# LayerNorm's statistics move from VectorE to TensorE and ScalarE, with a new order of work, in a two-layer image kernel

## The chip, the cores and the metric

The kernel runs on one core of a Trainium2 chip. The time is device microseconds of one execution, median of three runs. The engines are named as in the profile: PE (TensorE matmul), PEld (its weight load), DVE (VectorE), ACT (ScalarE), POOL (GpSimd) and SP (SyncE, which here only issues DMAs).

## The reference

Input x is four images of 192 channels x 128 x 128, float32. Two layers, each `x = x + f(groupnorm(x))`, with 32 groups of 6 channels. (The code calls them `layer0` and `layer1`; the text says layer 1 and layer 2.)

Layer 1: a 1x1 convolution to 48 channels; 16 of them go through a fractional Fourier transform, 16 through a real FFT, both with small convolutions on magnitude and phase; then a 1x1 convolution back to 192. Layer 2 is a state-space layer over the 16384 pixels of an image as a sequence:

```python
seq = (seq - mu) * rsqrt(var + 1e-5) * ln_g + ln_b        # over 192 channels
xs, z = split(seq @ in_proj_w.T, 2)                       # 384 and 384
u  = silu(causal_conv4(xs) + conv_b)
dt, Bm, Cm = split(u @ x_proj_w.T, [12, 28])              # 12, 16, 16
dt = softplus(dt @ dt_proj_w.T + dt_proj_b)
h[t] = h[t-1] * exp(dt[t] * A) + (dt[t] * u[t]) * Bm[t]   # 384 x 16 states
y = sum_s(h * Cm) + u * Dp
out = (y * silu(z)) @ out_proj_w.T
```

## The kernel before

**Layer 1.** `analysis(b)` loads an image in 16 pieces of 768 KB (`load`, L199), takes group statistics with `bn_stats` (L205), keeps the last 4 pieces, loads the other 12 again, multiplies by the scaled 1x1 weights (L301), evacuates (L305) and writes the result to DRAM (L311). `forward` reads it back with one DMA (L317) and transforms, `backward` transforms back, `synthesis` projects to 192 channels, adds x and writes `xmid` (L506, L510, L514). `weave` interleaves the four for different images. Image 0's analysis runs alone first. The last image's synthesis is interleaved with layer 2's prelude, two of its positions for one piece.

**Layer 2.** 128 chunks of 512 tokens (32 an image). A chunk has 24 positions: three tiles j of 128 channels times eight groups of two states. In each position `scans` (L977 on) runs two scans on DVE (L989), h = da*h + db. Then POOL multiplies both states of h by c (L1002, tile hc), and PE adds them up over the states while transposing (L1015, `sums`, three positions later). A DMA saves the last column of h (carry, L1000). The decay da = exp(dt*A) is ACT's (L911), made AHEAD states in advance. The input db = dt*u*B is made in one of three ways, set in KINDS for each position: V, a DVE product from PSUM (L932); O, a POOL product (L943), for which the decay goes to PSUM; P, ACT scales a transposed tile (L960, `scale`) and PE transposes it back (L975).

The rest of a chunk's work (normalization, convolution, projections, loads, gate, output) is put at fixed places by PLAN: an entry (-31, "A", "moments", 0) is done 31 positions before its chunk's first scan, in phase A of that position. A position's phases are S, A, M, L; the two scans begin after A, M lies between them, L after the carry. All queues work in order, so PLAN is the order written out by hand. SP's queue holds in this order the loads `load_b` and `load_c` (rows of B and C broadcast to 128 partitions, one buffer for each group), `load_x`, `load_xr`, the carries and the output. PSUM banks are handed out first in, first out (`psum`, `done`).

Normalization: `to_tokens` (L717) turns 512 tokens x 192 channels by a matmul with a diagonal matrix gd that holds the group norm's scale, and its shift in a 97th row that meets a row of ones in xm. `moments` (L732, L734) takes mean and variance on DVE from PSUM, `rstd` (L741 to L744) is Ln and two Exp on ACT (the second into PSUM for DVE), `shift` (L749) is DVE's -mean*rstd, and `normed` (L758) applies both on ACT. `group_norm` (L641 to L652) makes gd per image; the shift's row goes out to a DRAM tile and comes back as a row. `to_channels` and `channels` (L768, L784) turn back, and a DMA (L790) puts channels 128 to 191, moved by one token, into partitions 64 to 127 for the convolution (`conv`, L799). `proj_z` (L805, L806) computes z with two matmuls for each j; the second has 64 rows of weights and 64 of zeros.

## Time and profile before

| | us |
|---|---|
| median of 3 runs (10828.12 to 10840.17) | 10829.38 |
| profiled execution | 10830.13 |
| its span | 10828.4 |
| busy: PE, DVE, ACT, POOL | 9879.0, 10219.2, 9404.2, 9214.5 |
| first scan starts, last scan ends | 1395.10, 10811.20 |
| three costliest groups: POOL L1002, DVE L989 (first form), ACT L911 (first form) | 7202.9, 5821.6, 3423.7 |

The page gives busy time as a union: instructions that overlap by their pipelines count once. Start-to-start distances in a timeline are what an instruction really takes of a full engine. A line of waits is: engine and what waited, what released it, us in total, times, longest. A line of groups is: line, engine, operation, tiles, shape, count, busy us, mean ns. A timeline line is: start us, duration us, engine, line, operation, tiles and shape, count, and in brackets the idle time before it with what ended it. SPq and ACTq are queue issues.

### The profile page before, as it was taken

Reading aid. Unit: us, or ns where it says so; the run is one execution under the profiler, and the core shown is the slowest. Engines: PE = TensorE matmul, PEld = TensorE weight load, DVE = VectorE, ACT = ScalarE, POOL = GpSimd, SP = SyncE. Lnnn points to the kernel's source line nnn. Section 1 sums busy time; section 2 is a strip of 40 time slices with the busy share of each in tenths; the row PEclk is TensorE's granted clock in tenths of the full one; section 3 lists DMA queues with packets and bytes.
Section 4 is the critical chain, followed back from the end, with each engine's and each line's share of the span. In section 5 each row is a group of like instructions: output and inputs, shape, how many; then the busy total and the mean of one; then the engine's idle time right before and its main releaser. Section 6 shows DMA issues by size and latency. Waiting matters only on the chain.

```text
span 10828.4 us, 170277 instructions
## 1 busy us (share of the span) xinstructions
PE 9879.0 (91%) x55538; PEld 6942.9 (64%) x55538; DVE 10219.2 (94%) x11587; ACT 9404.2 (87%) x19559; POOL 9214.5 (85%) x4214
## 2 busy tenths in 40 slices
PE   4776789999999999999999999999999999999998
PEld 2444366666666666666666666666666666666666
DVE  4666699999999999999999999999999999999999
ACT  1332189999999999999999999999999999999998
POOL 0000089999999999999999999999999999999999
PEclk8888799999999999999999999999999999999999
DMA  8786743443443443443444444444444344344343
GB/s 229 189 227 179 222 137 108 126 127 108 127 124 111 124 125 112 122 126 112 120 127 113 118 127 116 115 127 118 113 127 122 109 127 123 109 127 126 108 127 98
DMA packets 1357320, 1416.75 MB, mean 131 GB/s; under 512 B 920729, under 2 KB 972174, under 8 KB 1355790
## 3 DMA queue, kind: packets, MB, share of 16 engines
q1 hardware_dynamic: 1335950, 1342.94, 44.5%
q0 software_dynamic: 13312, 50.34, 1.4%
q10 hardware_dynamic: 7168, 12.59, 0.4%
q8 instruction: 440, 7.21, 0.3%
q14 instruction: 450, 3.69, 0.1%
HBM read 1230.12 MB, written 155.33 MB: 128 GB/s over the span
## 4 chain that ended last, share of the span: by engine, by line
PE 50%; ACT 19%; DVE 17%; issue 5%; DMA 1%; POOL 0%; SPq 0%; DVEq 0%; POOLq 0%; ACTq 0%
PE ps L799 18%; PE ps L1015 14%; DVE h L989 11%; ACT da L911 6%; PE op L975 5%; DVE op L932 3%; PE ps L1055 3%; ACT dbT L960 3%; ACT L696 2%; ACT op L911 1%; ACT L818 1%; PE ps L1030 1%; ACT zs L818 1%; ACT sT L758 1%; DVE st L732 1%
## 5 line engine op out<-in xcount | busy, mean ns | idle before, releaser
L1002 POOL TENSOR_TENSOR hc<-h,c 128x1024 f32<-128x1024 f32 x3072 | 7202.9, 2367 | 314.5 <-DVE h L989 249.2
L989 DVE TENSOR_TENSOR_SCAN h<-da,carry,op 128x512 f32<-128x512 f32 x4712 | 5821.6, 1265 | 8.6 <-issue 2.9
L911 ACT ACTIVATE da<-dt,c_A_log 128x512 f32<-128x512 f32 x4864 | 3423.7, 751 | 219.5 <-DVE h L989 199.1
L1015 PE MATMUL ps<-ident,hc 128*128 128x128 f32 x24576 | 3221.3, 277 | 4.1 <-POOL hc L1002 4.1
L1015 PEld LDWEIGHTS ps<-ident,hc 128*128 128x128 f32 x24576 | 2866.7, 144 | 411.8 <-issue 402.0
L960 ACT ACTIVATE dbT<-ps,bT 128x128 f32<-128x128 f32 x8192 | 2291.2, 399 | 32.7 <-PE op L975 23.3
L799 PE MATMUL ps<-s,wc 128*128 128x512 f32 x4608 | 2142.3, 596 | 18.8 <-ACT s L784 13.9
L932 DVE TENSOR_TENSOR op<-ps,b 128x512 f32<-128x512 f32 x2816 | 1897.0, 674 | 5.7 <-ACT ps L892 5.7
L975 PE MATMUL op<-ident,dbT 128*128 128x128 f32 x8192 | 1319.6, 292 | 445.3 <-DVE h L989 417.9
L989 DVE TENSOR_TENSOR_SCAN h<-op,carry,db 128x512 f32<-128x512 f32 x1240 | 1547.3, 1267 | 6.9 <-ACT op L911 1.3
L943 POOL TENSOR_TENSOR db<-dtu,b 128x1024 f32<-128x1024 f32 x640 | 1514.1, 2366 | 6.2 <-DMA xmid<-xt 6.2
L975 PEld LDWEIGHTS op<-ident,dbT 128*128 128x128 f32 x8192 | 1034.0, 151 | 745.2 <-DVE h L989 437.3
L799 PEld LDWEIGHTS ps<-s,wc 128*128 128x128 f32 x4608 | 804.0, 190 | 725.0 <-issue 681.2
L911 ACT ACTIVATE op<-dt,c_A_log 128x512 f32<-128x512 f32 x1280 | 928.9, 726 | 14.1 <-DVE h L989 14.1
L1055 PE MATMUL ps<-yg,c_woT 128*96 128x512 f32 x1536 | 700.9, 592 | 0.0
L696 ACT ACT_TABLE_LOAD x511 | 655.6, 1283 | 9.8 <-PEq L1272 0.7
L514 POOL DMA_DIRECT2D xmid<-xt x64 | 41.7, 651 | 576.0 <-DVE xt L510 491.5
L857 POOL TENSOR_TENSOR dtu<-dt,u 128x512 f32<-128x512 f32 x384 | 482.5, 1271 | 0.0
L205 DVE BATCH_NORM_STATS2 st<-xt 96x6 f32<-96x512 f32 x512 | 322.6, 677 | 106.7 <-DMA xt<-in_x 105.5
L78 POOL TENSOR_TENSOR u<-u 128x1024 f32<-128x1024 f32 (+1 forms) x12 | 29.7, 2475 | 453.0 <-ACT u L77 453.0
L1055 PEld LDWEIGHTS ps<-yg,c_woT 128*96 128x96 f32 x1536 | 236.6, 163 | 273.1 <-issue 273.1
L1030 PE MATMUL ps<-ddp,u 128*128 128x128 f32 x3072 | 405.8, 275 | 0.0
(175 smaller groups left out, 10012.2 us busy)
## 6 DMA issues: line engine op xcount, KB each, us to landing
c<-dbc SPq DMA_DIRECT2D x1024, 512.0 KB, 4.9
b<-dbc SPq DMA_DIRECT2D x768, 512.0 KB, 6.1
xt<-in_x SPq DMA_DIRECT2D x176, 768.0 KB, 8.6
xmid<-xt POOLq DMA_DIRECT2D x64, 768.0 KB, 6.2
xm<-xmid SPq DMA_DIRECT2D x128, 384.0 KB, 3.9
carry<-h SPq DMA_DIRECT2D x3072, 1.0 KB, 2.0
xr<-xmid SPq DMA_DIRECT2D x128, 384.0 KB, 3.8
out<-xr SPq DMA_DIRECT2D x128, 384.0 KB, 3.9
```

The source lines that it names most:

```text
L696: nc.scalar.preload_act_table_set("natural_log_exp_and_others")
L799: nc.tensor.matmul(g["c", j][0], wc[:, j, k, :], rhs, start=k == 0, stop=k == 5)
L911: nc.scalar.activation(da, got[n]["dt", j], AF.Exp, scale=A[:, j, st : st + 1])
L932: nc.vector.tensor_tensor(dbs[s], g["dp", j][0], g["b", k % NG][:, q, :], ALU.mult)
L943: nc.gpsimd.tensor_tensor(db, _bc(g["dtu", j], 1, G), g["b", sg], ALU.mult)
L960: nc.scalar.activation(t[:, blk, :], g["tu", j][0][:, at], AF.Identity, scale=g["bT"][:, blk, st : st + 1],)
L975: nc.tensor.transpose(db[:, blk * 128 : (blk + 1) * 128], t[:, blk, :], ident)
L989: nc.vector.tensor_tensor_scan(h[:, q, :], das.pop(s), dbs.pop(s) if db is None else db[:, q, :], 0.0 if ch == 0 else g["before"][:, j, st ...
L1002: nc.gpsimd.tensor_tensor(hc, h, g["c", sg], ALU.mult)
L1015: nc.tensor.matmul(py[:, blk, :], hc[:, q, blk * 128 : (blk + 1) * 128], ident, start=first, stop=sg == NG - 1 and q == G - 1 and blk == N ...
L1030: nc.tensor.matmul(got[n]["py", j][0][:, blk * 128 : (blk + 1) * 128], got[n]["u", j][:, blk * 128 : (blk + 1) * 128], ddp[:, j, :], start ...
L1055: nc.tensor.matmul(po, woT[:, j, t * CH : (t + 1) * CH], g["yg", j], start=j == 0, stop=False)
```

## The change

In layer 2, gd becomes 192 columns wide and holds (identity - 1/192) times the group norm's scale, so that the two matmuls of a block add up in PSUM to values whose mean over channels is zero. `moments` becomes a Square on ACT with an accumulator output, which gives the variance; `shift` and the second Exp go; `normed` only scales. `group_norm` makes the shift's row by two small matmuls and an ACT copy, with no DRAM tile. `proj_z` for j = 1 and 2 runs its 64-row parts as a pair, one on partitions 0 to 63, the other on 64 to 127 (the moved copy). In layer 1 all 16 pieces of image 0 stay on chip in nine extra buffers, released before the other pools are made; the second pass takes pieces 10 to 15 and then 0 to 9. PLAN is rewritten, two positions in KINDS are exchanged in tiles 0 and 2, AHEAD goes from 5 to 6, hc from 5 to 4 buffers, zs from 5 to 4, dtu from 4 to 3.

```diff
-        def load(b, p):
+        def load(b, p, xp=xp):
-        def analysis(b, got):
+        def analysis(b, got, more=None):
+            keep = NPIECE if more else KEEP
-                xt = load(b, p)
-                if p >= NPIECE - KEEP:
+                xt = load(b, p, more if more and p < NPIECE - XBUFS else xp)
+                if p >= NPIECE - keep:
                     kept[p] = xt
...
-            for p in (*range(NPIECE - KEEP, NPIECE), *range(NPIECE - KEEP)):
+            last = NPIECE - (XBUFS // 2 * 2 if more else KEEP)
+            for p in (*range(last, NPIECE), *range(last)):
...
-        weave([(analysis(0, got[0]), 1)])
+        with tc.tile_pool(name="l0y", bufs=NPIECE - XBUFS) as more:
+            weave([(analysis(0, got[0], more), 1)])
...
-BUFS = 5, 4
-KINDS = ("VOPPVVVP", "OVVPVVOP", "VOVPPVOP")
+BUFS = 6, 4, 4, 4
+KINDS = ("VPOPVVVP", "OVVPVVOP", "VOVPVPOP")
...
-    (-37, "S", "load_x"), (-32, "A", "to_tokens", 0), (-32, "M", "to_tokens", 1),
+    (-44, "M", "load_x"), (-33, "S", "to_tokens", 0), (-33, "A", "to_tokens", 1),
...
-    (-2, "S", "turned", 0), (-2, "S", "load_b", 4), (-2, "A", "scale", 0, 5),
-    (-1, "S", "scale", 0, 7), (-1, "S", "load_b", 7), (-1, "A", "load_c", 4),
-    (-1, "M", "scale", 0, 6), (0, "S", "load_b", 6), (0, "S", "load_b", 2),
-    (0, "A", "scale", 0, 4), (1, "A", "load_b", 5), (1, "A", "load_c", 7),
+    (-1, "A", "scale", 0, 3), (-1, "M", "scale", 0, 2), (0, "S", "scale", 0, 6),
+    (0, "A", "load_b", 7), (0, "A", "scale", 0, 15), (0, "A", "load_b", 6), (0, "L", "load_b", 4),
+    (1, "S", "load_b", 3), (1, "A", "scale", 0, 7), (1, "A", "dt_u", 1), (1, "M", "scale", 0, 14),
+    (1, "L", "load_b", 5), (3, "L", "load_c", 4), (4, "S", "turned", 1), (4, "S", "load_c", 5),
...
-            nc.sync.dma_start(out=dnmr[:, b], in_=nmr[:, b])
+            for t in range(2):
+                nc.tensor.matmul(
+                    g["n",][0][0:1, 0:C], nmr[:, b, t : t + 1], centre[:, t, :],
+                    start=t == 0, stop=t == 1,
+                )
+            row = tp.tile([1, C], F32, name="nrow", bufs=1)
+            nc.scalar.copy(row, g["n",][0][0:1, 0:C])
+            nc.sync.dma_start(out=gd[CH : CH + 1, b, 0, :], in_=row)
             for t in range(2):
                 nc.vector.tensor_scalar(
-                    gd[0:CH, b, t, :], ident[0:CH, 0:CH], st2[:, b, t, 1:2], None, ALU.mult
+                    gd[0:CH, b, t, :], centre[:, t, :], st2[:, b, t, 1:2], None, ALU.mult
                 )
...
-                        row(g, blk)[:, t * CH : (t + 1) * CH],
-                        xm[:, t, blk * 128 : (blk + 1) * 128], gd[:, i // NCHUNK, t, :],
-                        start=True, stop=True,
+                        row(g, blk), xm[:, t, blk * 128 : (blk + 1) * 128],
+                        gd[:, i // NCHUNK, t, :], start=t == 0, stop=t == 1,
...
-                nc.vector.bn_stats(st[:, blk, :], row(g, 2 * half + blk))
-            for blk in range(2):
-                nc.vector.bn_aggr(g["mv"][:, 2 * half + blk, :], st[:, blk, :])
+                nc.scalar.activation(
+                    g["sT"][:, blk, :], row(g, blk), AF.Square, scale=C**-0.5,
+                    accum_out=g["mv"][:, blk : blk + 1],
+                )
...
-            nc.scalar.activation(g["rp"], lnv, AF.Exp, scale=-0.5)
...
-            nc.tensor.matmul(z, wz[:, 1, j, :], g["s"][:, 1, 3:], start=False, stop=True)
+            if j and ("z", 3 - j) not in g:
+                return
+            for h in (1, 2) if j else (0,):
+                rows = slice(64 * (h // 2), 64 * (h // 2 + 1)) if j else slice(0, 128)
+                nc.tensor.matmul(
+                    g["z", h][0], wz[rows, 1, h, :], g["s"][rows, 1, 3 + h // 2 :][:, 0:T],
+                    start=False, stop=True,
+                )
...
-            hc = scp.tile([128, G, T], F32, name="hc", bufs=5)
+            hc = scp.tile([128, G, T], F32, name="hc", bufs=HC)
```

## The prediction

> **What bounds the kernel now.** I read the page's slices first, then the waits of the steady stretch from 2000 to 9000 us by engine, then busy time in single chunks, then the timelines of one chunk by engine. The slices (270.7 us each; digits are tenths busy):
>
> ```profile
> PE   4776789999999999999999999999999999999998
> DVE  4666699999999999999999999999999999999999
> ACT  1332189999999999999999999999999999999998
> POOL 0000089999999999999999999999999999999999
> DMA  8786743443443443443444444444444344344343
> ```
>
> Five slices are layer 1, where DMA is busiest and nothing else is full; the rest is layer 2, where four engines are nearly full together. DVE's and POOL's waits there:
>
> ```profile
> DVE yg L1047 <- PE ps L1040: 21.2, 36, 1.1
> DVE h L989 <- issue: 3.6, 13, 0.5
> DVE h L989 <- ACT da L911: 2.6, 3, 0.9
> ...
> POOL hc L1002 <- DVE h L989: 176.4, 200, 1.5
> POOL hc L1002 <- PE ps L1015: 35.6, 91, 1.0
> ```
>
> In 7000 us, some 95 chunks, DVE waits about 31 us (0.33 a chunk); POOL, and ACT too, wait mostly for DVE's scans. Scans run from 1395.10 us to about 10811.2: 9416 us for 128 chunks, 73.56 each. Busy time in such a chunk (columns: length, then PE, PEld, DVE, ACT, POOL with instruction counts):
>
> ```profile
> 4072.00:4145.50 73.50, 70.06 (x410) 50.27 (x409) 73.19 (x83) 70.64 (x150) 71.30 (x33) 0.98 0.42 120
> ```
>
> So DVE sets the chunk, and the others follow at distances of 2 to 3 us. What DVE loses counts in full, until POOL at 71.3 or ACT at 70.6 plus what it gains is reached. Any wait given to DVE counts in full too.
>
> **The change, part by part.** The sum is made against the profiled execution: 10830.13 us, span 10828.4 and 1.7 around it; that is 0.75 us above the median of the runs, 10829.38.
>
> *DVE, per chunk.* Eight statistics instructions and the shift go:
>
> ```profile
> 4021.62 0.60 DVE L732 BATCH_NORM_STATS2 st<-ps 128x6 f32<-128x192 f32 x2
> 4022.14 0.30 DVE L734 BATCH_NORM_AGGREGATE mv<-st 128x2 f32<-128x6 f32 x2
> 4022.35 0.60 DVE L732 BATCH_NORM_STATS2 st<-ps 128x6 f32<-128x192 f32 x2
> 4022.87 0.30 DVE L734 BATCH_NORM_AGGREGATE mv<-st 128x2 f32<-128x6 f32 x2
> 4023.09 1.28 DVE L989 TENSOR_TENSOR_SCAN h<-op,carry,db 128x512 f32<-128x512 f32 x1
> ```
>
> Durations overlap, so I take start to start: 4023.09 - 4021.62 = 1.47 us, and the shift 4026.71 - 4026.64 = 0.07. Gain 1.54 us. Late next is POOL: 29 products of two states at about 2.33 us and three of one at 1.24 make 71.3, just under 73.56 - 1.54 = 72.02. The kinds keep their counts (11 V, 5 O, 8 P), so POOL, scans and products keep their work.
>
> *ACT, per chunk.* Before, the normalization ran from 4025.88 to 4028.43, 2.55 us, 0.33 of it waiting for the shift. After: Ln 0.35, one Exp 0.2, four scalings with one pointer operand. The one-pointer row is L960 (128 elements, 0.25 us start to start); 64 elements more at (0.613 - 0.25)/384 us each, from the 512-element Exp, give 0.31, so 1.25 for four. Added are four Squares with an accumulator output, which no row shows. Lower bound: a plain copy from PSUM start to start, 0.48 for 512, less 320 elements at 0.95 ns, so 0.18, 0.7 for four. Upper bound: the same plus a small ACT instruction for each result at 0.2 (L743), 1.5. I take 1.1, as nearest to no row but between both. Sum 2.9, so ACT gains 0.35 (0 to 0.75). It is hidden: ACT waits 150.0 us for DVE in those 95 chunks at L911, 1.6 a chunk. Without this cover it would cost the same 0.35. Table loads: in the new order of the plan, silu, exp and softplus still change eight times a chunk, so eight loads of 1.283 us as before; Square I take to need none, since in layer 1 L76 runs with no load put down to it.
>
> *PE, per chunk.* to_tokens keeps 16 records (a float32 matmul leaves two) of 192 instead of 96 columns: 1.76 us now; 192 x 0.43/512 = 0.16 each makes 2.58, so +0.82. proj_z falls from six 512-column products of 0.86 us to four and one pair on separate rows. The nearest row for a pair is L506 (49 rows at partition 0 and at 64): four records in 1.10 us, where two unpaired of L805 take 1.02. So 5.16 becomes 3.44 + 1.10 = 4.54: -0.62. Net +0.2, hidden: PE waits 301.1 us for DVE at L975, 3.2 a chunk. If the pair didn't overlap it would be +0.82, still covered.
>
> The Trainium skill's "TensorEngine Tiling (Array Packing)", Key Properties under Tiling Modes, speaks against this pair: a change of tiling mode drains TensorE. It gives no price. L506's 1.10 us lies inside a stream of 128-row products and so holds much of what the drain costs; by the rule in full PE would keep less of the 0.62, and DVE would lose nothing as long as PE still waits for it.
>
> *Buffers.* AHEAD 5 to 6 lets ACT run one decay further; hc 5 to 4, zs 5 to 4 and dtu 4 to 3 are nothing if PE and POOL stay as near to DVE as now: hc of position p needs the sums of p-4, which PE is given at p-1. POOL's wait for PE is 0.37 a chunk today and may grow by as much; its cover is 1.9 a chunk of waiting for scans.
>
> *DMA queue, per chunk.* The plan moves the loads of b and c. SP works in order and issues a load only behind the carry of the position before, which waits for a scan:
>
> ```profile
> 4039.02 0.60 SPq L1000 DMA_DIRECT2D carry<-h  x1
> 4039.66 0.60 SPq L877 DMA_DIRECT2D b<-dbc  x1
> ...
> DMA to landing us min/median/max: 4.7/5.9/7.3
> ```
>
> Group 4 of b was asked for at position -2; now it stands at 0, phase L, behind the carry of position 0. Its first product is in position 3, after one scan: positions 1 and 2 at 2.36 and a scan of 1.18, 5.9 us after position 0's end. Carry 0.64 and a landing of 5.9 make 6.5. DVE would wait 0.6 a chunk, from none (4.7 landing) to 2.0 (7.3). Queued behind the waiting product are all later scans. I take 0.4, because ACT's and POOL's lag moves DVE's own positions later. Group 5 has 7.1 us for the same 6.5. Group 4 of c, now at 3, L, has one position (3.5 us) plus POOL's lag of some 2 us against 0.64 + 4.9: even, taken as nothing, at most 1 on POOL. load_x moves to -44 (eleven positions early) and hides.
>
> *Layer 1, image 0.* Twelve reloads of 768 KB go. The second pass starts at 75.65; PE needs 1.94 us a piece (L301), so 16 end at 106.7 instead of about 117. Copy 1.26, write issue 0.8, landing 5.9 (best of the crowded landings) bring the last write to 114.7; the image load took 139.64 - 128.87 = 10.8. The transform would start at 125.5 instead of 139.64: -14. Everything after shifts with it. Bounds: 0 (ACT's 25.1 us of waiting for writes stay) and -20 (writes land at 3 us, image load at 8).
>
> *Between the layers.* The shift rows go to a DRAM tile and back:
>
> ```profile
> 1250.16 12.65 SPq L650 DMA_DIRECT2D gd<-dnmr  x2
> ...
> 1274.28 7.56 PE L506 MATMUL pr<-cat,w2x 49*96 49x512 f32 x16 [16.77 <-DMA cat<-dimg]
> ```
>
> That issue holds SP while the cat loads wait behind it until 1271.72. They can't run before dimg has landed (1249.67 + 13.9 = 1263.6). The new path is two small PE products, one ACT copy and one DMA of one row per image, each in series as the row has one buffer. Gain 6 (0 to 8). Against it, the plan starts at -44 instead of -37 with two positions per synthesis step, so seven more positions come after synthesis, among them proj_dt, softplus (3.0 with its load) and to_tokens (2.6). DVE waited for ACT there anyway (5.67 and 4.83), so I take +3 (-3 to 15).
>
> Sum: 128 x (-1.54 + 0.4) = -146; start -14 - 6 + 3 = -17. 10828.4 - 163 = 10665 span, 10667 in all; I say 10665.
>
> **The rivals.** (A) As above, DVE still the bound: 10665, from 10563 (no DVE waits left, -1.54 - 0.33 a chunk, start -28) to 10700.
>
> (B) ACT becomes the bound. Its chunk without waits for DVE is 73.56 - 1.6 = 71.96; with 0.75 from dear accumulator reads and 0.2 of new waits for PE, 72.9: 128 x 72.9 + start 1378 + tail 17 + 2 = 10728. For it: ACT is 96% busy. Against: spaced back to back, its decays take 0.613, not the 0.72 of the isolated ones, so its busy time shrinks under load.
>
> (C) POOL becomes the bound with its idle time as it is: 71.17 + 2.4 = 73.56 as before, and only the start is gained: 10813. Against: most of that idle time is for scans, which come earlier.
>
> (D) Slower: the b load of group 4 at position 0. The point is 1.67 us of DVE wait a chunk ((128 x 1.54 + 17)/128). The longest landing gives 2.0 to 2.1, with group 6 asked for one position before and xr right behind it on the same engines: 128 x 0.56 - 17 = +55, 10885. For it: no slack in the plan, a queue that starts the load only at a scan's end. Against: the median landing gives 0.6.
>
> The skill's "DMA: Bandwidth & Descriptors", Anatomy of one DMA, puts a transfer on the GpSimd path at 2.0 us plus its bytes over 436 GB/s; as an estimate from it, 512 KB would be 3.2 us and D would vanish. The landing row says 4.7 at best, and the sum goes by the row.
>
> **How the numbers follow.** A 0.58, B 0.20, C 0.07, D 0.15. Faster than 0.2% (some 22 us, what the measurement can tell) are A and B: 0.78; C is within: 0.07; D slower: 0.15. The range 10575 to 10850 holds A but its edge, B and C, and leaves out D. A's own range is 10575 to 10700.
>
> **What would show it.** Right: DVE rows without BATCH_NORM on 128x192; chunks near 72.4; POOL's wait for scans under 1 a chunk; the transform of image 0 starting near 125; no SP issue of 12 us between the layers. D shows as DVE products L932 waiting for DMA b; B as scans waiting for da or dbT; C as scans waiting for hc. The prediction is wrong if chunks stay above 73.5, by any DVE wait over 1.5 us that repeats each chunk, or if DVE's small instructions were already hidden so that the chunk shrinks by under 1 us with no new wait.

## The result and the profile after

The changed kernel takes 10750.35 us, the median of 4 runs (10746.81 to 10752.18); the kernel before took 10828.75 in the runs beside it. The ratio is 0.9928, 95% interval 0.9911 to 0.9945: 0.72% faster, 78 us. The forecast was 10665 us, 1.5% faster. The direction held and the time lies in the range; half of the gain did not come. One execution of the run with five steps moved (experiment 4) took 24990.86 us at a granted clock of 0.454, and its time there is the median of the other five.

The profiled execution (10746.81 us, span 10744.7) splits against the one of before like this. The first scan starts at 1356.75 us instead of 1395.10, 38.4 earlier (forecast 17). The last scan ends at 10726.70: 9369.95 us for 128 chunks, **73.20 a chunk instead of 73.56** (forecast 72.42), 46 us in all instead of 146. The tail is 0.8 us longer.

Busy time in one chunk of the changed kernel, in the columns of the row shown before (PE, PEld, DVE, ACT, POOL):

```profile
4072.00:4145.20 73.20, 71.10 (x410) 50.78 (x409) 71.31 (x74) 71.24 (x158) 71.22 (x33) 0.98 0.40 119
```

VectorE went from 73.19 to 71.31: the work is gone, as forecast. But the chunk is 73.20, so VectorE now idles 1.9 us in it, and all four engines stand within 0.3 us of one another. The waits from 2000 to 9000 us (total, times, longest), some 95.6 chunks, engine by engine:

```profile
DVE h L1000 <- ACT op L922: 163.8, 192, 2.0
...
DVE op L943 <- DMA b<-dbc: 1.8, 6, 0.4
...
ACT dbT L971 <- PE op L986: 59.0, 94, 0.8
ACT da L922 <- DVE h L1000: 51.1, 115, 0.9
...
PE ps L875 <- ACT dt L861: 95.0, 95, 1.0
PE ps L771 <- ACT sT L762: 82.1, 96, 0.9
PE op L986 <- ACT dbT L971: 54.0, 41, 1.5
PE op L986 <- DVE h L1000: 38.6, 37, 1.5
...
POOL hc L1013 <- DVE h L1000: 77.8, 162, 1.5
POOL hc L1013 <- DMA c<-dbc: 66.6, 67, 2.7
```

The waits for scans in the same stretch of the kernel before, some 95.2 chunks:

```profile
ACT da L911 <- DVE h L989: 141.7, 190, 1.0
...
ACT op L911 <- DVE h L989: 8.3, 13, 0.7
...
PE op L975 <- DVE h L989: 301.1, 123, 3.4
```

Three things are to be seen. VectorE's new wait is for `op`, a decay that ScalarE writes into a PSUM bank for positions of kind O: 192 times, twice a chunk, 1.71 us a chunk. Before, ScalarE waited 1.6 us a chunk for VectorE's scans and TensorE 3.2; now it is 0.53 and 0.40. And the wait for `b` that the forecast charged with 0.4 is 0.02.

The two places, in the timeline of VectorE and of ScalarE (start, length; x the count; in brackets the idle time before and its releaser):

```profile
4059.91 1.27 DVE L1000 TENSOR_TENSOR_SCAN h<-op,carry,db 128x512 f32<-128x512 f32 x1
4062.39 1.28 DVE L1000 TENSOR_TENSOR_SCAN h<-op,carry,db 128x512 f32<-128x512 f32 x1 [1.22 <-ACT op L922]
4073.46 1.28 DVE L1000 TENSOR_TENSOR_SCAN h<-op,carry,db 128x512 f32<-128x512 f32 x1 [0.38 <-ACT op L922]
...
4027.13 0.73 ACT L922 ACTIVATE da<-dt,c_A_log 128x512 f32<-128x512 f32 x1 [0.44 <-DVE h L1000]
...
4048.77 0.37 ACT L746 ACTIVATE sT<-ps 128x192 f32<-128x192 f32 x1
4048.98 0.25 ACT L746 ACTIVATION_READ_ACCUMULATOR sT<-ps 128x1 f32 x1
4049.07 0.38 ACT L746 ACTIVATE sT<-ps 128x192 f32<-128x192 f32 x1
...
4050.20 0.30 ACT L756 ACTIVATE lnv<-mv,eps 128x4 f32<-128x4 f32 x1
...
4059.52 2.25 ACT L971 ACTIVATE dbT<-ps,bT 128x128 f32<-128x128 f32 x8
4061.52 0.84 ACT L922 ACTIVATE op<-dt,c_A_log 128x512 f32<-128x512 f32 x1
...
4087.67 1.14 ACT L971 ACTIVATE dbT<-ps,bT 128x128 f32<-128x128 f32 x4 [0.64 <-PE op L986]
```

The second scan of position 22 of the chunk waits 1.22 us for a decay that stands behind eight scalings (L971, `scale 2 14` and `2 15` of the plan). The second place is position 2, behind `scale 0 7`. Between the two bracketed ScalarE rows, 4027.13 and 4087.67, no row of ScalarE has a wait: it is behind through 60 of 73 us, not at one instruction. The squares with their accumulator reads take 4048.77 to 4050.20, 1.43 us; Ln, Exp and the four scalings of the rows 1.79.

The chain that ended last, by engine, in the changed kernel (before: PE 50%, ACT 19%, DVE 17%):

```profile
PE 45%; ACT 32%; DVE 11%; issue 3%; DMA 1%; POOL 0%; SPq 0%; DVEq 0%; POOLq 0%; ACTq 0%
```

ScalarE's share grew by 13 points. TensorE's is the largest in both, though before VectorE hardly waited; the run without the skip products (experiment 3) shows what such a share is worth.

At the start, SyncE's timeline shows the load of the first two transformed images (before: 128.87 and 276.37) and the shift rows between the layers:

```profile
126.37 0.81 SPq L315 DMA_DIRECT2D img<-d  x1
240.58 0.70 SPq L315 DMA_DIRECT2D img<-d  x1
...
1228.53 0.56 SPq L663 DMA_DIRECT2D gd<-nrow  x1
...
1234.38 0.50 SPq L663 DMA_DIRECT2D gd<-nrow  x1
```

Image 0's own load came 2.5 us earlier, not 14; image 1's 35.8; the third and fourth keep 29.8 and 31.9 (496.58 and 773.76 against 526.42 and 805.65). The three shift rows follow one another within 6 us, where one issue had held SyncE for 12.65.

### The profile page after: what moved, and what is told of

It is laid out like the page before. It is cut to its first block, busy times and chain, and to the rows that moved or that the text cites. A ratio compares the mean times of both kernels' runs of the same rounds, so it can differ in the third digit from the quotient of the medians.

```text
span 10744.7 us, 171310 instructions
## 1 busy us (share of the span) xinstructions
PE 9930.4 (92%) x55554; PEld 6885.5 (64%) x55554; DVE 9996.6 (93%) x10439; ACT 9485.3 (88%) x20458; POOL 9234.1 (86%) x4214
## 4 chain that ended last, share of the span: by engine, by line
PE 45%; ACT 32%; DVE 11%; issue 3%; DMA 1%; POOL 0%; SPq 0%; DVEq 0%; POOLq 0%; ACTq 0%
PE ps L802 17%; PE ps L1026 12%; ACT da L922 9%; DVE h L1000 8%; ACT dbT L971 5%; PE op L986 5%; ACT op L922 3%; ACT L711 3%; DVE op L943 2%; PE ps L1041 2%; ACT dt L861 2%; ACT sT L762 2%; ACT sT L746 1%; PE ps L732 1%; ACT L829 1%
## 5 line engine op out<-in xcount | busy, mean ns | idle before, releaser
L1000 DVE TENSOR_TENSOR_SCAN h<-da,carry,op 128x512 f32<-128x512 f32 x4712 | 5796.3, 1263 | 1.3 <-issue 0.8
L1026 PE MATMUL ps<-ident,hc 128*128 128x128 f32 x24576 | 3161.1, 275 | 3.9 <-POOL hc L1013 3.9
L1026 PEld LDWEIGHTS ps<-ident,hc 128*128 128x128 f32 x24576 | 2831.5, 142 | 416.8 <-issue 368.3
L971 ACT ACTIVATE dbT<-ps,bT 128x128 f32<-128x128 f32 x8192 | 2333.7, 423 | 89.5 <-PE op L986 79.3
L1000 DVE TENSOR_TENSOR_SCAN h<-op,carry,db 128x512 f32<-128x512 f32 x1240 | 1571.3, 1267 | 211.6 <-ACT op L922 207.3
L986 PE MATMUL op<-ident,dbT 128*128 128x128 f32 x8192 | 1289.6, 277 | 151.7 <-DVE h L1000 75.6
L986 PEld LDWEIGHTS op<-ident,dbT 128*128 128x128 f32 x8192 | 968.6, 141 | 512.0 <-ACT dbT L971 221.6
L732 PE MATMUL ps<-gd,xm 97*128 97x192 f32 x2048 | 433.2, 360 | 0.0
```

What stands on the lines that cost most here:

```text
L971: nc.scalar.activation(t[:, blk, :], g["tu", j][0][:, at], AF.Identity, scale=g["bT"][:, blk, st : st + 1],)
L986: nc.tensor.transpose(db[:, blk * 128 : (blk + 1) * 128], t[:, blk, :], ident)
L1000: nc.vector.tensor_tensor_scan(h[:, q, :], das.pop(s), dbs.pop(s) if db is None else db[:, q, :], 0.0 if ch == 0 else g["before"][:, j, st ...
L1026: nc.tensor.matmul(py[:, blk, :], hc[:, q, blk * 128 : (blk + 1) * 128], ident, start=first, stop=sg == NG - 1 and q == G - 1 and blk == N ...
```

## The experiments

All start from the changed kernel unless said otherwise. "Chunk" is the time from the start of the first scan to the end of the last over 128; "idle" is the part of a chunk in which VectorE is not busy, by its busy share from 2000 to 9000 us. By that rule the kernel before has 73.56 and 0.46, the changed one 73.20 and 1.82. Both come from one profiled execution of each kernel; the first run below has the same layer 2 as the kernel before, and its chunk is 73.558 where the kernel before has 73.563. The start scatters much more: among the nineteen kernels that share the changed layer 1 the first scan starts between 1348.60 and 1378.71 us, so kernels are compared by their chunks. The theories were T1, the order of ScalarE's queue; T2, the amount of ScalarE's work; T3, TensorE or POOL; and later T4 to T8, named where they come up.

**1. Layer 1 alone** (from the kernel before, with only the hunks of the change that lie in the first layer).

```diff
-        weave([(analysis(0, got[0]), 1)])
+        with tc.tile_pool(name="l0y", bufs=NPIECE - XBUFS) as more:
+            weave([(analysis(0, got[0], more), 1)])
...
-            for p in (*range(NPIECE - KEEP, NPIECE), *range(NPIECE - KEEP)):
+            last = NPIECE - (XBUFS // 2 * 2 if more else KEEP)
+            for p in (*range(last, NPIECE), *range(last)):
...
```

> The kernel before with only the layer-1 part of the change: image 0 kept on chip during its statistics, the other pools opened after it. The first scan came 38.35 us earlier in the changed kernel (1395.10 to 1356.75), the transform of image 0 only 2.4 us earlier. If the loads that are saved let image 1's statistics run ahead: load of image 1's transform near 241 us instead of 276, first scan near 1360, chunk as before 73.56, 10793 us in all. If the gain at the start came from the shift row or the plan: first scan 1380 to 1395 and 10813 to 10829 us.

10797.98 us, ratio 0.9975 (0.9966 to 0.9984); chunk 73.56. The loads of the transformed images come at 125.40 and 244.24, and the first scan at 1371.29, 23.8 earlier. So the saved loads hardly shorten image 0: ScalarE still waits 1.2 to 7.6 us at a time for the writes of its products (`d<-x`), as it did before (1.3 to 7.2). They let image 1's statistics start at 83.36 us instead of 118.10, beside image 0, and that lead stays. From the start of layer 2's setup (the load of `c_ln`) to the first scan it is 148.73 us before, 149.94 here, 145.30 in the changed kernel. These 3 to 5 us are not shown to come from the rest of the change: in the other runs the same stretch takes 137.92 to 153.07 us. The setup itself starts at 1246.37 us before, at 1221.35 here, and between 1202.05 and 1227.53 in all nineteen kernels with the changed layer 1, so its gain lies between 19 and 44 us.

**2. The order at the two decays; the squares left out; the variance back on VectorE.**

```diff
-    (1, "A", "scale", 0, 7), (1, "A", "dt_u", 1), (1, "M", "scale", 0, 14),
+    (1, "A", "dt_u", 1), (1, "M", "scale", 0, 7), (1, "M", "scale", 0, 14),
...
-    (21, "S", "scale", 2, 14), (21, "A", "scale", 2, 15),
+    (21, "M", "scale", 2, 14), (21, "L", "scale", 2, 15),
```

> The changed kernel with three scalings of dbT moved behind the decay that they stood in front of in ScalarE's queue: scale (0,7) from position 1, phase A, to M; scale (2,14) and (2,15) from position 21, phases S and A, to M and L. No work is added or removed. T1 (order: VectorE's 1.71 us of waiting a chunk for op decays comes from what stands before those two decays): the waits fall under 0.4 a chunk, the chunk from 73.2 to 72.0 to 72.4 (POOL's 71.4 busy and its 0.7 of waiting for c set the floor), 1357 + 128 x 72.2 + 20 = about 10620 us in all. T2 (amount: ScalarE has 71.3 us of work and some 1.5 of waits that do not go away): the wait moves to other decays, chunk 73.0 to 73.3, 10720 to 10755 us.

10808.94 us, ratio 0.9983 (0.9973 to 0.9992), chunk 73.69, idle 2.00: slower than the changed kernel. VectorE's waits at the decays are gone to the last one, and two others stand in their place:

```profile
DVE h L1000 <- PE op L986: 89.6, 188, 1.4
DVE op L943 <- ACT ps L903: 77.8, 95, 0.9
```

VectorE now waits for TensorE's transposes of the later scalings, and for the copy of `dt u` (L903), which ScalarE reaches later. T1 in its simple form falls.

```diff
-                g["mv"] = tp.tile([128, NBLK], F32, name="mv")
+                g["mv"] = ones
...
-                nc.scalar.activation(
-                    g["sT"][:, blk, :], row(g, blk), AF.Square, scale=C**-0.5,
-                    accum_out=g["mv"][:, blk : blk + 1],
-                )
```

> The changed kernel without the sums of squares: Ln reads a constant tile of ones, so LayerNorm's variance is left out of the computation. ScalarE loses 1.43 us a chunk, VectorE, POOL and PE nothing. T1 and T2 (ScalarE behind, by order or by amount): VectorE's waits for op decays fall by about 1.4 us a chunk, chunk 71.8 to 72.2, 10570 to 10625 us. T3 (ScalarE is not what holds the chunk; PE's unbroken 35 us or POOL's wait for c do): chunk 72.8 to 73.2, 10695 to 10750 us.

10715.21 us, ratio 0.9895 (0.9879 to 0.9912), chunk 72.94, idle 1.22. ScalarE lost 1.24 us of busy time a chunk, the chunk 0.27. So the amount of ScalarE's work alone (T2) is not what holds the chunk. Of the 1.71 us of waiting at the decays 0.80 are still there (95.97 chunks):

```profile
DVE h L997 <- ACT op L919: 77.2, 189, 0.7
```

```diff
-                nc.scalar.activation(
-                    g["sT"][:, blk, :], row(g, blk), AF.Square, scale=C**-0.5,
-                    accum_out=g["mv"][:, blk : blk + 1],
-                )
+                nc.vector.bn_stats(st[:, blk, :], row(g, 2 * half + blk))
...
+                nc.vector.bn_aggr(g["mv"][:, 2 * half + blk, :], st[:, blk, :])
...
```

> The changed kernel with the variance computed by VectorE again (bn_stats and bn_aggr over the already centred rows), everything else as changed, the new plan among it. VectorE gains 1.47 us of work a chunk (71.4 to 72.8), ScalarE loses 1.43. T2 (ScalarE bound in the changed kernel by its amount of work): its waits go, VectorE is the bound again, chunk 72.9 to 73.2, 10710 to 10750 us: moving the statistics was worth almost nothing. If VectorE's waits stay as they are, whatever ScalarE has to do (T3): 73.2 + 1.47 = 74.7, about 10935 us.

10953.18 us, ratio 1.0117 (1.0102 to 1.0132), chunk 74.75. VectorE's work is at 73.28, about as before, but it idles 1.48 instead of 0.46, and that with ScalarE at 70.2:

```profile
DVE h L1000 <- ACT op L922: 74.7, 185, 0.6
DVE st L747 <- PE ps L732: 26.3, 57, 1.2
```

So with the rest of the change in place, moving the statistics off VectorE is worth 1.55 us a chunk, all that was forecast; and the rest of the change, the new order among it, costs 1.2 against the kernel before when the statistics stay. The wait at the decays is again 0.80 a chunk (74.7 us in 93.6). So of the changed kernel's 1.71 some 0.8 come with the new order, wherever the statistics are, and some 0.9 with the squares on ScalarE.

**3. The old order; TensorE relieved; both relieved; POOL's wait taken away.**

```diff
-KINDS = ("VPOPVVVP", "OVVPVVOP", "VOVPVPOP")
+KINDS = ("VOPPVVVP", "OVVPVVOP", "VOVPPVOP")
...
-    (-44, "M", "load_x"), (-33, "S", "to_tokens", 0), (-33, "A", "to_tokens", 1),
+    (-37, "S", "load_x"), (-32, "A", "to_tokens", 0), (-32, "M", "to_tokens", 1),
...
```

> The changed kernel with the order and the kinds of before put back (PLAN and KINDS; the step shift is gone, the numbers of buffers stay as changed). Work of every engine is the same as in the changed kernel. T4 (the new order makes the waits: 1.8 us of VectorE's idle time a chunk come from where the new plan puts steps): VectorE's waits near the 0.5 of before, chunk 71.8 to 72.4, with a first scan near 1360 in all 10570 to 10645 us. T5 (any order has such waits, because ScalarE at 71.3, PE at 70.2 and POOL at 71.4 no longer have room to answer VectorE in time): waits 1.3 to 2.3 a chunk, chunk 72.8 to 73.7, 10695 to 10810 us.

10970.31 us, ratio 1.0140 (1.0123 to 1.0156), chunk 75.02, idle 3.59:

```profile
DVE yg L1059 <- PE ps L1052: 276.2, 94, 3.0
DVE h L1001 <- ACT op L923: 29.3, 93, 0.4
```

The waits at the decays nearly go (0.31 a chunk), as T4 has it, but the gate's wait for the transposes of `yt` grows from 0.22 us a chunk in the kernel before to 2.96. The old order does not fit the changed work, and the changed order not the old work. The numbers of buffers stayed as changed here, and POOL's wait for TensorE's sums, 0.37 a chunk before, is 0.78 (73.2 us in 93.3): a part of this run's price may be theirs.

```diff
                     sums(*order[pos - LAG])
-                    add_skip(n, j)
```

> The changed kernel without the products that add the skip D u to y (add_skip is left out of the computation). PE loses 2.67 us a chunk (three times eight records, 0.89 each), nothing else changes. In the chain that ended last PE runs without a gap for 35 of the 73 us of a chunk. If PE's work is what makes VectorE wait (T3): chunk 71.7 to 72.3, 10560 to 10635 us. If PE is only late because others are (T5 in its form that ScalarE is first): chunk 72.8 to 73.2, 10695 to 10750 us.

10755.91 us, ratio 0.9937 (0.9922 to 0.9952), chunk 73.19, idle 1.81: nothing. TensorE's busy time falls from 70.23 to 68.01 and its wait for VectorE's scans grows instead (in the profiled execution, 10768.14 us, the first scan starts 22 us later than in the changed kernel, at 1378.71; its chunks are the same):

```profile
PE op L986 <- DVE h L1000: 182.7, 115, 1.8
...
DVE h L1000 <- ACT op L922: 163.5, 192, 1.6
```

> The changed kernel without the sums of squares and without the skip products: ScalarE loses 1.43 us and PE 2.67 us a chunk. Without the squares alone the chunk fell by 0.27 only, and VectorE still waited 1.2. T5 (VectorE waits because ScalarE and PE answer late together): waits under 0.5, chunk 71.5 to 72.0, 10530 to 10600 us. T4 (the waits belong to the order: a decay behind two scalings, whatever the load): waits stay near 1.0, chunk 72.3 to 72.8, 10635 to 10700 us.

10676.85 us, ratio 0.9866 (0.9851 to 0.9880), chunk 72.60, idle 1.07. The edit is the squares' and the skip's together. Alone they give 0.27 and 0.02, together 0.60, so either engine seems to hold the chunk where the other is relieved; and with both relieved 0.80 us of waiting at the decays are still there (76.6 us in 96 chunks).

```diff
-    (3, "L", "load_c", 4),
+    (2, "S", "load_c", 4),
```

> The changed kernel with c's load for group 4 asked for at position 2, phase S, instead of 3, L. POOL waits 0.70 us a chunk for c in the changed kernel. If POOL with 71.4 busy and this wait is part of what holds the chunk: chunk 72.5 to 72.9, 10655 to 10710 us. If POOL follows the others: its wait for c goes and its wait for scans grows by as much, chunk 73.1 to 73.3, 10735 to 10760 us.

10738.93 us, ratio 0.9922 (0.9908 to 0.9937), chunk 73.14. POOL's wait for c is gone and its wait for scans went from 77.8 to 140.2 us: POOL follows.

**4. Order and load together; two more steps out of the way.**

> The changed kernel with both earlier edits: the three scalings behind the two decays, and the sums of squares left out (Ln reads ones, so the variance is left out of the computation). Alone, the order cost 0.48 us a chunk and the squares' absence gained 0.27. T6 (VectorE waits at two places for two causes together, the scalings ahead of the decay and a ScalarE that arrives late; with ScalarE 1.43 us earlier the scalings still reach PE in time): waits under 0.6, chunk 71.8 to 72.3, 10570 to 10635 us. T5 (ScalarE's order only chooses who is late, TensorE's transposes or the copy of dt u instead of the decay): waits 1.2 to 2.0, chunk 72.6 to 73.4, 10670 to 10775 us.

10739.85 us, ratio 0.9914 (0.9899 to 0.9929), chunk 73.11, idle 1.38: the edits are those of the order and of the squares. T6 falls: VectorE waits 0.80 us a chunk for TensorE's transposes and 0.31 for the copy of `dt u`.

What remains of ScalarE's lag can be read in the run without squares. There ScalarE itself waits 0.44 us for a scan to free the bank, so it is on time, and the next decay is still late:

```profile
4051.59 0.69 ACT L919 ACTIVATE op<-dt,c_A_log 128x512 f32<-128x512 f32 x1 [0.44 <-DVE h L997]
4052.22 0.71 ACT L919 ACTIVATE da<-dt,c_A_log 128x512 f32<-128x512 f32 x1
4052.84 2.15 ACT L968 ACTIVATE dbT<-ps,bT 128x128 f32<-128x128 f32 x8
4054.83 0.74 ACT L919 ACTIVATE op<-dt,c_A_log 128x512 f32<-128x512 f32 x1
...
4055.60 1.28 DVE L997 TENSOR_TENSOR_SCAN h<-op,carry,db 128x512 f32<-128x512 f32 x1 [0.53 <-ACT op L919]
```

The banks called op are three, each scan frees one, and the decay for the scan three states on takes it. ScalarE can't run ahead of the written order, because each da also waits for a scan's buffer. Where no product stands between the scans, such a decay has two scans, 2.4 us, for itself and all that is written before it: here 0.61 of da, 2.0 of scalings and 0.7 of its own. The theory T8 made of this was tried with five steps moved and then one more:

```diff
-    (-2, "L", "dtu_copy", 0),
+    (-3, "M", "dtu_copy", 0),
...
-    (0, "A", "scale", 0, 15), (1, "A", "scale", 0, 7), (3, "L", "load_c", 4), (21, "A", "scale", 2, 15),
+    (1, "M", "scale", 0, 7), (1, "M", "scale", 0, 15), (2, "S", "load_c", 4), (21, "M", "scale", 2, 15),
```

> The changed kernel with five steps moved, no work added or removed: scale (2,15) behind the decay of state 22 (position 21, phase A to M), the copy of dt u for block 0 directly behind it (position 22, L, to 21, M), scale (0,15) and (0,7) behind the decay of state 2 (positions 0 and 1, A, to 1, M), and c's load for group 4 at position 2. T8 (a decay into an op bank has two scans, 2.4 us, from the freeing of its bank to its own scan; 2.05 us of scalings in front of it are the wait): VectorE's waits 0.4 to 1.0 a chunk, chunk 71.9 to 72.5, 10580 to 10660 us. T5 (ScalarE is late through this stretch in any order, and the wait only changes its place): waits 1.5 to 2.3, chunk 72.9 to 73.7, 10705 to 10810 us.

10769.46 us, ratio 0.9943 (0.9931 to 0.9956), chunk 73.37, idle 1.62. The decays' wait fell to 0.14 a chunk (13.8 us in 95.4), and the load of b that the forecast had charged came up in its place:

```profile
DVE op L944 <- DMA b<-dbc: 67.3, 75, 2.1
...
DVE h L1001 <- ACT op L923: 13.8, 40, 0.7
```

VectorE does not come to this load's product earlier than in the changed kernel; the load lands later. The issue of the load and its product, first in the changed kernel, then here:

```profile
4070.23 0.60 SPq L888 DMA_DIRECT2D b<-dbc  x1
...
4075.83 0.68 DVE L943 TENSOR_TENSOR op<-ps,b 128x512 f32<-128x512 f32 x1
...
2022.99 0.98 SPq L889 DMA_DIRECT2D b<-dbc  x1
...
2030.07 0.70 DVE L944 TENSOR_TENSOR op<-ps,b 128x512 f32<-128x512 f32 x1 [1.25 <-DMA b<-dbc]
```

In 48 chunks between 2000 and 9000 us of each, the changed kernel's load lands a median of 4.4 us after its issue (4.1 to 6.0) and VectorE is ready for it at 5.6; here it lands at 6.5 (4.5 to 7.7) and VectorE is ready at 5.8. It is issued 2.1 us after the load before it instead of 2.9 (4070.23 after 4067.33); that this crowding makes it land later is not shown.

```diff
-    (0, "A", "load_b", 6), (0, "L", "load_b", 4),
+    (0, "A", "load_b", 4), (0, "L", "load_b", 6),
```

> The five moved steps of the run before, and b's loads for groups 4 and 6 exchanged (4 at position 0, A, 6 at 0, L), so that group 4 is asked for one position, some 2.1 us, earlier. T8 (a list of places that can be worked off one by one): the wait for b goes, 0.71 us, and the chunk falls from 73.37 to 72.5 to 72.8, 10655 to 10700 us. T5 (the next wait takes its place): chunk 73.0 to 73.4, 10720 to 10775 us.

10748.60 us, ratio 0.9930 (0.9916 to 0.9943), chunk 73.22, idle 1.41: the time of the changed kernel, with six steps elsewhere and another list of waits:

```profile
DVE h L1001 <- PE op L987: 51.7, 138, 1.3
DVE op L944 <- DMA b<-dbc: 29.9, 43, 1.6
...
DVE h L1001 <- ACT op L923: 11.0, 31, 1.0
```

The listed waits are 1.3 us a chunk here against 1.8 in the changed kernel, at the same chunk. The rest is probably gaps too short to see: VectorE's busy time reads 71.8 a chunk instead of 71.4 for the same work, and a scan's row (1263 to 1268 ns in both) is some 0.09 us longer than the distance from one scan's start to the next where they follow one another (four in 4.70 us from 4067.12), so a gap up to that size would read as busy.

**5. The kinds of positions.**

```diff
-KINDS = ("VPOPVVVP", "OVVPVVOP", "VOVPVPOP")
+KINDS = ("VPOPVVVP", "OVVPVVOP", "VOVPPVOP")
...
-    (18, "M", "scale", 2, 10), (19, "S", "turn", 1), (19, "M", "scale", 2, 11),
+    (18, "M", "scale", 2, 8), (18, "M", "scale", 2, 9), (19, "S", "turn", 1),
...
-    (-28, "S", "to_channels", 1),
+    (-28, "L", "to_channels", 1),
```

> As the one before, but only the third block's kinds are those of before (VOVPPVOP); state 2 keeps P, O, P. T7: the larger wait (1.2 of 1.7 us a chunk, state 22) goes and the one at state 2 stays or grows: chunk 72.2 to 72.8, 10620 to 10695 us. T5: 72.8 to 73.6.

("The one before" is the run with all the old kinds, which follows.) 10817.20 us, ratio 0.9991 (0.9981 to 1.0000), chunk 73.74, idle 2.01. The decays' waits are still 1.38 a chunk (131.1 us), and TensorE's transposes add 0.44. T7 falls for the larger of the two places.

> The changed kernel with the kinds of before (VOPPVVVP, OVVPVVOP, VOVPPVOP) in the new order; the scalings follow the positions that are now of kind P, and the transposes of the second LayerNorm half stand one half position later to have a PSUM bank. Work of every engine as changed. T7 (the waits come from the neighbours P, O, P at states 2 and 22, where VectorE runs three positions without a product and ScalarE has four scalings and six decays): VectorE's waits under 0.9 a chunk, chunk 71.9 to 72.4, 10580 to 10645 us. T5 (some wait of 1.2 to 2 a chunk stays whatever the order): 72.8 to 73.6, 10695 to 10800 us.

10993.12 us, ratio 1.0154 (1.0138 to 1.0169), chunk 75.04. The first block's kinds are put back too, with its scalings 3 and 2 becoming 5 and 4. This run does not decide what it was made for: ScalarE's busy time is 73.88, 2.6 more than in the changed kernel, and in 150 us there are 20 table loads instead of 17. A position of kind O in the first block's third place asks for no decay ahead, so the silu of u and of z beside it share one table; with kind P there, exp comes between them. The kinds of that block were tied to the tables.

> The kinds of before and no sums of squares (Ln reads ones, the variance is left out of the computation). T7: with ScalarE 1.43 us shorter the rest of the waits goes too, chunk 71.6 to 72.0, 10540 to 10590 us. T5: waits of 1.0 to 1.5 stay, 72.5 to 73.0, 10655 to 10720 us.

10778.81 us, ratio 0.9954 (0.9940 to 0.9969), chunk 73.46, with ScalarE at 72.60 and idle for 0.86 only: the same pair of loads, less the squares. Here ScalarE is close to being the bound, and this is what that looks like: taking the squares away cut 1.28 us of its busy time and 1.58 off the chunk, where the same edit to the changed kernel, in which it idles 1.92, gave 0.27.

**6. The pair of z products.**

```diff
-                rows = slice(64 * (h // 2), 64 * (h // 2 + 1)) if j else slice(0, 128)
+                rows = slice(0, 64) if j else slice(0, 128)
...
-                    g["z", h][0], wz[rows, 1, h, :], g["s"][rows, 1, 3 + h // 2 :][:, 0:T],
+                    g["z", h][0], wz[rows, 1, h, :], g["s"][rows, 1, 3 : T + 3],
```

> The changed kernel with the two 64-row products of z on the same rows 0 to 63, so that they follow one another. If the pair overlapped, PE gains 0.6 to 0.8 us a chunk. Since PE has no part in the chunk (2.67 us less of it changed nothing): chunk 73.1 to 73.3, time within 20 us of the changed kernel. If PE is just at the edge and has room below but none above: chunk 73.4 to 73.9, 10770 to 10835 us.

10792.90 us, ratio 0.9970 (0.9958 to 0.9981), chunk 73.55, idle 2.18. The four records of 64 rows take 1.06 us to the next product's start in the changed kernel (the first two lines) and 1.92 here:

```profile
4028.76 1.13 PE L814 MATMUL ps<-s,wz 64*128 64x512 f32 x4
4029.82 0.65 PE L1051 MATMUL ps<-ident,yt 128*128 128x128 f32 x4
...
4041.11 1.98 PE L814 MATMUL ps<-s,wz 64*128 64x512 f32 x4
4043.03 0.66 PE L1051 MATMUL ps<-ident,yt 128*128 128x128 f32 x4
```

The pair overlaps, as forecast, and is worth 0.34 us a chunk. 0.86 us more of TensorE at this place cost that; the skip products' 2.67 us (2.22 of busy time) elsewhere had given nothing. In this run ScalarE waits 25.3 us for the products that feed softplus (L861), a wait that the changed kernel doesn't have: the pair stands in TensorE's queue ahead of the products for softplus, near the start of ScalarE's long stretch; that this is why its place matters is a reading, not shown.

**7. A pair of table loads saved** (the second run adds `scale 0 7` and `2 15` behind the decays and the earlier load of c, the third `scale 2 14` too). The silu of z for two blocks was moved beside the silu of u, z's products two to three positions earlier, and the output products and their copies later to free the banks.

```diff
-    (9, "M", "proj_z", 2), (11, "S", "proj_z", 1), (11, "S", "silu_z", 1), (11, "M", "silu_z", 2),
+    (7, "M", "proj_z", 2), (8, "S", "proj_z", 1), (8, "M", "silu_z", 1), (8, "M", "silu_z", 2),
...
-    (31, "M", "project_out", 1), (33, "M", "project_out", 0), (34, "A", "add_x", 0), (34, "L", "add_x", 1),
+    (33, "M", "project_out", 1), (33, "L", "project_out", 0), (34, "L", "add_x", 0), (35, "A", "add_x", 1),
```

> The changed kernel with the silu of z for blocks 1 and 2 moved next to the silu of u for block 2 (z's products from positions 9 and 11 to 7 and 8, the silu from 11 to 8, the output products and their copies one to two positions later to free PSUM banks). One pair of table loads goes (silu and back to exp, 2.56 us of ScalarE a chunk); the result is the reference's. T6: ScalarE has room, but the decay of state 22 still stands behind two scalings: chunk 72.5 to 72.9, 10655 to 10710 us. If ScalarE's amount alone were the cause: 71.6 to 72.1, 10545 to 10605 us. T5: 73.0 or more.

> The same, with scale (0,7) and scale (2,15), but not (2,14), moved behind the decays, and c's load for group 4 at position 2. T6: both causes are gone, waits under 0.5, chunk 71.6 to 72.1, 10545 to 10605 us. T5: a wait for PE's transposes or for the copy of dt u takes over, chunk 72.5 to 73.2.

> The same with (2,14) moved behind the decay too, as in the first order experiment. T6: as the one before within 0.3 of a us a chunk, 71.6 to 72.2, 10545 to 10620 us, since ScalarE's 2.56 us less let the scalings reach PE in time. T5: PE's transposes of state 23 wait as they did in the first order experiment (0.95 a chunk), and VectorE for them, chunk 72.6 to 73.5.

11264.38, 11283.08 and 11331.57 us, ratios 1.0394 (1.0377 to 1.0412), 1.0414 (1.0397 to 1.0432) and 1.0463 (1.0447 to 1.0478); chunks 76.92, 77.36 and 77.70. ScalarE's busy time did fall, to 68.9, but none of the theories is told apart: the copy of the output (`xr`) now stands right behind its product and stops ScalarE's queue for 2.6 us a chunk (in the first of the three), and VectorE stands for 4.0 behind it:

```profile
DVE h L1000 <- ACT xr L1073: 365.4, 91, 5.7
```

That is an error in the moved steps. It shows the price of a wait in an in-order queue: 2.6 us of ScalarE's standing cost more than the two table loads had held.

**What is settled.** VectorE's work fell by 1.73 us a chunk and 1.36 of it came back as idle time. It is not ScalarE's work alone that brings it, nor TensorE's, nor POOL's wait for c, nor the few steps in front of the two decays: with any one of these taken away the chunk stays between 72.9 and 73.7, with other waits. Only relieving ScalarE and TensorE together moved it further, to 72.60. The runs support the reading that, at 70.2 to 71.4 us of work on four in-order engines, the waiting for one another is what holds 73.2. Open are the 1.07 us that remain in that run, where POOL (71.25 busy) was not relieved, and whether an order made anew would do better; no full order was tried. No run changed the numbers of buffers. In the changed kernel POOL waits 0.8 us in all for TensorE's sums, which speaks against the fifth `hc` buffer being missed there; of `zs`, `dtu` and AHEAD nothing is shown.

## Why the prediction was right or wrong

*VectorE, -1.54 a chunk: right.* Busy time fell by 1.73 (73.11 to 71.38), and putting the work back cost 1.55.

*ScalarE, +0.35, "It is hidden": the failing step, together with the order that was taken at nothing (below).* The size was in its bounds: 0.68 of busy time, of which the squares 1.43 where 1.1 was taken. The cover was wrong. The forecast set ScalarE's 1.6 us and TensorE's 3.2 us of waiting for scans against the new work, but these were waits for the engine that the change makes faster. They had to shrink by VectorE's own gain, 1.54, before anything new was laid on them: 1.6 - 1.54 - 0.35 is below nothing. The forecast counted the gain in full and the cover in full, and they were the same microseconds. What came instead is 0.53 and 0.40 of these waits, and VectorE waiting 1.71 for ScalarE. The subtraction does not account for all of it: with the measured 0.68, ScalarE by itself would set 73.56 - 1.58 + 0.68 = 72.66 a chunk, about half of the way from the 72.02 that VectorE's gain alone leaves to the 73.20 that came. The rest is the order and the engines' waits for one another, and the runs do not split it further.

*TensorE, +0.2, hidden: size nearly right (+0.37), cover gone for another reason.* Here the subtraction leaves room: 3.16 - 1.54 - 0.37 is 1.25 us of waiting for scans. But only 0.40 came, while TensorE's listed waits for ScalarE grew from some 0.5 to 2.4 us a chunk (95.0, 82.1 and 54.0 us): it now waits for the engine that is late. to_tokens takes 2.72 us (1.41 and 1.31) where 2.58 was forecast, the pair 1.06 where 1.10 was. That the pair would be worth nothing while TensorE waits is refuted by the unpaired run, 0.34 us a chunk. The Trainium skill's "TensorEngine Tiling (Array Packing)", Key Properties under Tiling Modes, says that a change of tiling mode drains TensorE; 0.2 us would fit that, by which the pair exceeds the 0.86 of a full overlap and the four unpaired records exceed 1.72, but no run here shows that the drain is what takes them.

*Buffers and order: "nothing", and for the order wrong.* The order was read for loads on SyncE's queue and not for what stands before the decays on ScalarE's. With the statistics on VectorE the new order and the rest cost 1.2 us a chunk, and the old order with the new work costs 1.8 more than the new one. So the new order is needed for the new work and is not free; its 0.80 us at the decays stand without the squares too, where the old order has 0.31.

*b's load, +0.4: wrong at this kernel, 0.02, and right about the mechanism.* The term that was off is the landing: 5.9 us was taken from the kernel before, and this load lands after 4.4. VectorE's lag did little: it is ready 5.6 us after the issue, where the forecast's 5.9 from position 0's end less 0.64 for the carry make 5.26. With five steps moved VectorE is ready at 5.8, the load lands after 6.5, and the wait is 0.71 us a chunk, near the 0.6 that the forecast had from its landing of 5.9.

*c's load, "at most 1 on POOL": right*, 0.70, and harmless.

*Table loads: right*, eight a chunk and none for Square.

*Start, -17: the size was wrong.* Image 0 was charged with -14 on its own transform; that gained 2.5 (0.3 to 6.6 in the nineteen kernels with this layer 1, at 122.26 to 128.62 us), and the gain is the lead of image 1's statistics, 30 to 36 us at the later images. Between the layers -6 and +3 were forecast, and 3.4 us came (148.73 to 145.30), which is not clear of the scatter of that stretch.

*The rivals.* B, ScalarE as the bound at 72.9 a chunk and 10728 us, was nearest in time and named the right waiter and the right engine waited for. But its mechanism, ScalarE as the one bound by its amount of work, is refuted by the run without squares: 1.24 us less gave 0.27. That its time came so near is in part luck. Neither A nor B held the case that came: several engines nearly full that make one another wait, with none the bound. C and D did not come.

## What to carry to other kernels

Idle time in which an engine waits for the one that is being relieved is no cover: it shrinks by the same amount as the relief, so subtract the gain from it first, and only then lay new work on it. When four engines come within a few per cent of the span, adding up the bound's work is not enough: go through each in-order queue at the places with the least room, for what is moved out of the way of one wait arrives late somewhere else. A chain that names an engine for 45% of the span need not be what holds it: the run that left out 2.67 us a chunk of that engine's products gained nothing, so other chains must have been about as long.

## What the runs showed of the hardware

An accumulator output on ScalarE is an instruction of its own in the trace, ACTIVATION_READ_ACCUMULATOR: a Square of 128x192 from PSUM and its read take 0.30 us from start to start, of which the read 0.09. A product over 64 rows costs as much as one over 128 when nothing runs beside it (1.92 us against 1.72 for four records of 512 columns) and little more than half when its partner is on the other rows (1.06). The loads of `b`, 512 KB each, had a median of 4.7 us from issue to landing in the changed kernel and 5.9 in the run with five steps moved. And layer 1, the same in nineteen kernels, reached the setup of layer 2 between 1202.05 and 1227.53 us: up to 25 us at the start are not a difference between kernels.
